# Top-2 experts: every expert on every token, or each token to its two experts only

## The chip, the cores and the metric

The kernel runs on one core of a Trainium2 chip. Times are device microseconds (us) of that core for one execution. The time before is the median of 3 runs, 867.42 us (864.79 to 869.43). The profile is of one further execution.

## The reference

The input is x, 8 sequences of 512 tokens with 128 features, all in float32. One causal attention layer with 16 heads of 8 features is followed by a layer normalization, then a mixture of 14 experts, then a second layer normalization:

```python
x = _layernorm(x + attention(x))          # 16 heads, head size 8, causal
t = x.reshape(4096, 128)
probs = softmax(t @ gate_w.T)             # (4096, 14)
top2_p, top2_i = top_k(probs, 2)
w = top2_p / top2_p.sum(-1)
hh = gelu(einsum('nd,edf->nef', t, w1) + b1)      # F = 256, exact gelu
all_out = einsum('nef,efd->ned', hh, w2) + b2     # all 14 experts
moe = w[:, 0] * all_out[n, top2_i[:, 0]] + w[:, 1] * all_out[n, top2_i[:, 1]]
x = _layernorm(x + clip(t + moe, -100, 100))
```

Only two of the 14 expert outputs of a token have a weight; the reference computes all and picks two.

## The kernel before

**Layout.** Tokens are tiles of 128 on the partitions: NQ = 4 tiles to a sequence, NT = 32 in all. The input x_sb, the attention result y_sb and all weights stay on chip. SP's queue carries the loads in the order of the code: x_sb (L71), the expert weights w1_sb and w2_sb (L101, L102), then everything that attention moves. The small weights and biases go on ScalarE's queue (L68 to L95). GpSimd (POOL) sets constants at the start.

**Attention** is written in an order of its own, by `tc.manual_schedule()`: instructions stay in program order on each engine. A unit u is four heads of one sequence, so there are NU = 32 units, 4 to a sequence, and a unit is UN = 5 steps. A loop over steps s calls `front(u, i)` for step s and `back(u, i)` for step s - 12 (LAG). Everything else is put on a step by `at(step, fn, ...)` into the table `jobs` and called after front and back of that step. `front` computes scores (L287) and a mask (L297) into PSUM and takes row maxima on VectorE. `shift_pieces` and `shift_rows` (L350 to L364) send the maxima as three bf16 rows into the operand qr, by a transfer on SP. `back` recomputes the transposed scores with the shift (L376), takes the exponential on ScalarE (L411), and POOL sets the masked part to zero (`select`, L387). `product` (L433) multiplies with the values, two or three steps after `back`. `evacuate`, `divide`, `project` and `residual` finish a unit or a sequence: the last adds the projection to x (L497) and takes the statistics of the layer normalization (L157, L158). `load_xT`, `split` (L248 to L260) and `load_rows` (L270, L277) prepare the next sequence: queries and keys are split into three bf16 pieces, stored to a scratch in DRAM and read back as rows.

**Experts.** After the last sequence, `layernorm_rstd` computes all scales at once, and a loop over the 8 sequences normalizes (L564), transposes (L572) and computes the router's logits (L575). The choice of the two experts is made for all 32 tiles in some 20 VectorE operations (L594 to L617) that end in w_all, a weight for every token and expert, zero for all but two. Then two nested loops, over 8 sequences c and 14 experts e, call `expert_in` (two matmuls L649 of 128 by 512 and two GELUs L653) one expert ahead of `expert_out` (eight matmuls L661 of 128 by 128, accumulated in PSUM in pairs, and four multiply-adds L669 on VectorE into acc). In the trace every float32 matmul is two entries (two passes), so L661 counts 1,792 and L649 448. `start` adds the biases b2 through a matmul (L633), `end` clips, adds, and takes statistics. After the last expert the second normalization runs over all tiles (L711), and SP stores each sequence (L719).

Of the kernel before, what the change touches and what calls it, by code (L numbers as in the profile page):

```python
# [12 lines left out]
BF = mybir.dt.bfloat16  # L13

# [14 lines left out]
LOWEST = -3.0e38  # L29


@with_exitstack
def kernel(
# [24 lines left out]
    SCALE = 1.0 / float(D) ** 0.5  # L58

# [37 lines left out]
    w1_sb = const.tile([P, E, F], FP, tag="w1_sb", name="w1_sb")  # L97
    w2_sb = const.tile([P, E, NFC, D], FP, tag="w2_sb", name="w2_sb")
    half = E // 2
    for lo, hi in ((0, half), (half, E)):  # L100
        nc.sync.dma_start(w1_sb[:, lo:hi, :], w1[lo:hi].rearrange("e d f -> d e f"))  # L101
        nc.sync.dma_start(  # L102
            w2_sb[:, lo:hi, :, :].rearrange("p e c d -> p (e c) d"),
            w2[lo:hi].rearrange("e (c p) d -> p (e c) d", p=P),
        )


    eps = const.tile([P, 1], FP, tag="eps", name="eps")
    nc.gpsimd.memset(eps, LN_EPS)
# [17 lines left out]
    for e in range(E):  # L127
        nc.gpsimd.memset(rank[:, e : e + 1], float(E - e))

# [20 lines left out]
    y_sb = const.tile([P, NT, D], FP, tag="y_sb", name="y_sb")  # L150
# [9 lines left out]
    def layernorm_rstd(pool, n):  # L160
        std = pool.tile([P, NT], FP, tag="std", name=f"std_{n}", bufs=1)
        rstd = pool.tile([P, NT], FP, tag="rstd", name=f"rstd_{n}", bufs=1)
        nc.scalar.activation(std, stats[:, :, 1], AF.Sqrt, bias=eps)
        nc.vector.reciprocal(rstd, std)
        return rstd
# [10 lines left out]
    with tc.tile_pool(name="work", bufs=2) as work, tc.tile_pool(  # L176
# [309 lines left out]
        def residual(b):  # L486
            aT, xb = outs.pop(("a", b))
            op = bank(f"op_{b}")
            for qb in range(NQ):
# [8 lines left out]
                y_sb[:, b * NQ : (b + 1) * NQ, :].rearrange("p t d -> p (t d)"),  # L498
                op,
                xb.rearrange("p t d -> p (t d)"),  # L500
                ALU.add,
            )
            for qb in range(NQ):
                layernorm_stats(work, y_sb[:, b * NQ + qb, :], b * NQ + qb)


        def step_of(u, i):
            return u * UN + i

# [11 lines left out]
        for u in range(NU):  # L521
# [10 lines left out]
            if g == NG - 1:  # L532
                at(k + 9, project, b)
                at(k + 11, residual, b)

        last = max(jobs)
        for s in range(-1, last + 1):
# [8 lines left out]
    with tc.tile_pool(name="big", bufs=1) as big, tc.tile_pool(  # L546
        name="ffn", bufs=2
    ) as ffn, tc.tile_pool(
        name="ps_t", bufs=2, space=bass.MemoryType.PSUM
    ) as ps_t, tc.tile_pool(  # L550
# [143 lines left out]
        for c in range(B):  # L694
            for e in range(E):
                hT = expert_in(c, e)
                if e == 0:
                    start(c)
# [66 lines left out]
```

## Time and profile before

| what | value |
|---|---|
| median of 3 runs | 867.42 us |
| the profiled execution | 868.49 us |
| its span, first to last instruction | 866.8 us |
| TensorE matmul busy | 775.2 us (89%) |
| TensorE weight load busy | 491.8 us (57%) |
| VectorE busy | 440.4 us (51%) |
| ScalarE busy | 372.0 us (43%) |
| POOL busy | 170.3 us (20%) |
| mean granted TensorE clock | 0.953 |
| DRAM read, written | 25.09 MB, 8.39 MB |

PE is TensorE's matmul, PEld its weight load, DVE VectorE, ACT ScalarE, POOL GpSimd, and SPq or ACTq the issue of a transfer on that queue. A group of instructions reads: line, engine, operation, output<-input, sizes, count | busy us, mean ns of one | idle us of the engine just before them, with what ended it. A matmul's own duration overlaps its neighbour's, so the beat of a repeated group in the chain says more than its mean. A stretch table gives the busy time of every engine between two times, and after it the granted clock (1.00 is full speed), the share of the DMA engines in use and GB/s.

### The profile page before, as it was taken

The numbers are of one execution on the slowest core, as the hardware profiler recorded it, in microseconds if no ns is written. First come the engines' busy times: TensorE is split into PE (matmuls) and PEld (weight loads), VectorE is DVE, ScalarE is ACT, GpSimd is POOL, SyncE is SP. The second block draws the span as 40 slices with busy tenths as digits, with TensorE's granted clock in tenths as the row PEclk, the third lists the DMA queues.
The fourth block names the chain that finished last, engine by engine and source line by source line (L and its number), as shares of the span: only waits on it lengthen the run. The fifth ranks groups of instructions, "written<-read, shape, count | busy, mean of one in ns | idle before, by whom it ended". The sixth has DMA issues, their size and how long they took to land.

```text
span 866.8 us, 13255 instructions
## 1 busy us (share of the span) xinstructions
PE 775.2 (89%) x5118; PEld 491.8 (57%) x5118; DVE 440.4 (51%) x996; ACT 372.0 (43%) x497; POOL 170.3 (20%) x455
## 2 busy tenths in 40 slices
PE   1489989989898999998698999999999999999992
PEld 0244444545454454554475777777777777777772
DVE  5275765666766674773446343434334343433436
ACT  0025544455565654567352443333333334344331
POOL 3133534354444443444100000000000000000000
PEclk9969997999999996999698999999999999999996
DMA  8531213122222221110000000000000000000003
GB/s 234 165 117 52 89 49 92 57 65 79 66 67 71 75 75 48 56 30 2 2 1 1 1 1 1 1 0 1 1 1 1 1 1 1 1 1 1 1 1 97
DMA packets 31060, 34.72 MB, mean 40 GB/s; under 512 B 5812, under 2 KB 26390, under 8 KB 30998
## 3 DMA queue, kind: packets, MB, share of 16 engines
q1 hardware_dynamic: 29632, 33.44, 12.8%
q8 instruction: 40, 0.66, 0.3%
q10 hardware_dynamic: 1366, 0.45, 0.2%
q14 instruction: 22, 0.18, 0.1%
HBM read 25.09 MB, written 8.39 MB: 39 GB/s over the span
## 4 chain that ended last, share of the span: by engine, by line
PE 84%; DVE 6%; ACT 4%; DMA 2%; issue 2%; POOL 1%; SPq 0%; ACTq 0%; POOLq 0%; DVEq 0%
PE op L661 23%; PE hp L649 21%; PE f L287 10%; PE av L433 9%; PE b L376 9%; PE f L297 3%; ACT pt L411 2%; PE tr L450 1%; PE op L490 1%; PE bp L633 1%; PE logits_ps L575 1%; DVE x_sb L711 1%; PE q L248 1%; DMA gate_nat<-in_L_ffn_gate_w_dram 1%; PE mt L360 1%
## 5 line engine op out<-in xcount | busy, mean ns | idle before, releaser
L653 ACT ACTIVATE hT<-hp,b1T 128x512 f32<-128x512 f32 x224 | 153.6, 687 | 247.9 <-PE hp L649 222.8
L661 PEld LDWEIGHTS op<-w_sb,hT 128*128 128x128 f32 x1792 | 218.1, 192 | 53.2 <-issue 30.1
L669 DVE SCALAR_TENSOR_TENSOR acc<-op,w_all,acc 128x128 f32<-128x128 f32 x448 | 126.0, 344 | 227.0 <-PE op L661 227.0
L661 PE MATMUL op<-w_sb,hT 128*128 128x128 f32 x1792 | 219.1, 275 | 0.0
L411 ACT ACTIVATE pt<-b 128x1024 f32<-128x1024 f32 x160 | 163.4, 1023 | 129.4 <-PE b L376 125.5
L649 PE MATMUL hp<-yT,w_sb 128*128 128x512 f32 x448 | 211.7, 595 | 0.4 <-ACT hT L653 0.4
L287 PE MATMUL f<-kr,qr 72*128 72x384 bf16 (+3 forms) x512 | 122.2, 323 | 8.4 <-DMA qr<-qsc 8.4
L387 POOL TENSOR_SCALAR_AFFINE_SELECT pt<-pt 128x256 f32<-128x256 f32 (+1 forms) x224 | 95.2, 439 | 157.5 <-ACT pt L411 144.6
L334 DVE TENSOR_REDUCE part<-f 128x8 f32<-128x1024 f32 x64 | 78.3, 1224 | 62.2 <-PE f L297 61.1
L649 PEld LDWEIGHTS hp<-yT,w_sb 128*128 128x128 f32 x448 | 76.9, 192 | 55.2 <-issue 53.2
L287 PEld LDWEIGHTS <-qr 72*128 72x128 bf16 x512 | 47.9, 103 | 103.8 <-issue 84.3
L376 PE MATMUL b<-qr,kr 75*128 75x384 bf16 (+3 forms) x512 | 100.8, 311 | 0.4
L433 PE MATMUL av<-pt,v_aug 128*32 128x512 f32 (+3 forms) x1024 | 94.2, 464 | 0.9 <-POOL pt L387 0.9
L341 DVE TENSOR_REDUCE mx<-f 128x2 f32<-128x1024 f32 x64 | 78.0, 1221 | 31.0 <-PE f L297 31.0
L297 PE MATMUL f<-causal_bf,ident_bf 128*128 128x256 bf16 (+1 forms) x320 | 85.8, 268 | 0.0
L376 PEld LDWEIGHTS <-kr 75*128 75x128 bf16 x512 | 46.2, 101 | 22.6 <-issue 8.3
L433 PEld LDWEIGHTS av<-pt,v_aug 128*32 128x32 f32 x1024 | 24.2, 111 | 42.0 <-issue 26.6
L329 DVE TENSOR_REDUCE mx<-f 128x4 f32<-128x1024 f32 x32 | 39.0, 1219 | 11.6 <-PE f L297 11.6
L297 PEld LDWEIGHTS <-ident_bf 128*128 128x128 bf16 x320 | 33.2, 104 | 12.3 <-issue 3.2
L360 PE MATMUL mt<-ident_bf,mp 128*48 128x128 bf16 x32 | 7.3, 227 | 28.4 <-DVE krest L252 12.6
L443 ACT COPY oT<-av 128x512 f32<-128x512 f32 x32 | 18.7, 584 | 19.2 <-PE av L433 19.1
L450 PE MATMUL tr<-ident,oT 128*128 128x128 f32 x128 | 20.6, 286 | 1.2 <-ACT oT L443 1.2
(109 smaller groups left out, 402.8 us busy)
## 6 DMA issues: line engine op xcount, KB each, us to landing
kr<-ksc SPq DMA_DIRECT2D x32, 288.0 KB
qr<-qsc SPq DMA_DIRECT2D x96, 96.0 KB
w_sb<-in_L_ffn_w_dram SPq DMA_DIRECT2D x4, 896.0 KB
qsc<-qpc SPq DMA_DIRECT2D x24, 128.0 KB
ksc<-kpc SPq DMA_DIRECT2D x24, 128.0 KB
x_sb<-in_L_attn_x_dram SPq DMA_DIRECT2D x8, 256.0 KB
out_dram<-x_sb SPq DMA_DIRECT2D x8, 256.0 KB
qr<-mt SPq DMA_DIRECT2D x96, 4.0 KB
```

What stands on the lines that cost most here:

```text
L287: nc.tensor.matmul(ps[:, col : col + W], qr[u % RING][0:KR, j, qb * P : (qb + 1) * P], kr[u % RING][0:KR, j, :W], start=first, stop=False, ...
L297: nc.tensor.matmul(out, ident_bf, causal_bf[:, 0:n, :], start=False, stop=True, skip_group_check=True,)
L334: nc.vector.reduce_max(part[:, j : j + 2, :], ps.rearrange("p b (s k) -> p b s k", k=P), axis=AX.X,)
L341: nc.vector.reduce_max(mx[:, j : j + 2, 3], ps, axis=AX.X)
L376: nc.tensor.matmul(ps[:, col : col + W], kr[u % RING][:, j, kb * P : (kb + 1) * P], qr[u % RING][:, j, kb * P :], start=first, stop=True, ...
L387: nc.gpsimd.affine_select(out=view, in_=view, pattern=[[0, k] for k in n] + [[1, P]], compare_op=ALU.is_ge, fill=0.0, base=0, channel_mult ...
L411: nc.scalar.activation(pt, ps, AF.Exp, scale=SCALE)
L433: nc.tensor.matmul(avs[u][HS * j : HS * (j + 1), kb * P :], v_aug[b % 2][:, kb, g * GH + j, :], p, start=(kb == 0), stop=(kb == NQ - 1),)
L649: nc.tensor.matmul(hp, w1_sb[:, e, f * P : (f + 1) * P], yT[:, c, :], start=True, stop=True)
L653: nc.scalar.activation(hT[:, f, :], hp, AF.Gelu, bias=b1T[:, k : k + 1])
L661: nc.tensor.matmul(op[:, i, :], hT[:, f, i * P : (i + 1) * P], w2_sb[:, e, f, :], start=(f == 0), stop=(f == NFC - 1),)
L669: nc.vector.scalar_tensor_tensor(acc[:, i, :], op[:, i, :], w_all[:, c * NQ + i, e : e + 1], acc[:, i, :], op0=ALU.mult, op1=ALU.add,)
```

## The change

Each token's row goes to its two experts only, through DRAM.

- **Routing per sequence.** `route(b)` is a generator; `proceed` runs one piece of it per step, from two steps after `residual` of that sequence. It normalizes on ScalarE (scale and shift from POOL), transposes, computes logits, takes the two best experts on VectorE, and counts with small matmuls (a strictly lower triangle and ones) at which row of its expert each token stands, with the running counts in `place`. The weights of the two experts come from one exponential and a power on POOL.
- **Scatter.** Each row is 130 numbers: 128 features, the weight, and where the result goes. Eight indirect transfers per sequence (4 tiles, 2 choices), each of 128 rows, go from POOL's queue into XS in DRAM, two per step.
- **Fill.** After the second to last sequence is counted, SP loads 14 places into registers and writes 768 rows behind each expert's rows, so that whole blocks can be read. The last sequence's first scatter waits for these.
- **Weights.** The expert weights aren't loaded on chip any more; at step 5 SP copies them within DRAM into WP, 514 numbers to a row, with the biases b1 at the end.
- **Blocks.** A plan on VectorE gives each of NBLK = 45 blocks of 256 tokens its first row in XS, its expert and how many of its rows count. SP loads row and expert of a block into registers and then its tokens and weights, four blocks ahead. A block is transposed, multiplied, passed through GELU, multiplied again, weighted on VectorE and scattered by two indirect transfers of 128 rows from POOL to OS; rows that don't count have a place outside and are left out.
- **End.** OS is read back in two halves per sequence, by SP and ScalarE. POOL adds the first, VectorE the second, and the rest is done for each sequence: clip, sum, statistics, scale on POOL, normalization on ScalarE, store.

The diff, cut to its core:

```diff
-    w1_sb = const.tile([P, E, F], FP, tag="w1_sb", name="w1_sb")
-    w2_sb = const.tile([P, E, NFC, D], FP, tag="w2_sb", name="w2_sb")
...
+    NBLK = (2 * N + E * (BT - 1)) // BT
...
+    def layernorm_scale(pool, c, n):
...
+        nc.gpsimd.tensor_scalar(rstd, stats[:, ts, 1], LN_EPS, 1.0, ALU.add, ALU.mult)
+        nc.gpsimd.tensor_tensor(rstd, rstd, powers[:, 0], ALU.pow)
+        nc.gpsimd.tensor_tensor(shift, stats[:, ts, 0], rstd, ALU.mult)
+        nc.gpsimd.tensor_scalar(shift, shift, -1.0, 0.0, ALU.mult, ALU.add)
...
+    def scatter(key, dst, idx, src, bound):
+        inst = nc.gpsimd.indirect_dma_start(
+            dst,
+            bass.IndirectOffsetOnAxis(ap=idx, axis=0),
+            src,
+            None,
+            bounds_check=bound,
+            oob_is_err=False,
+        )
...
+        def pack_weights():
+            wide = WP.rearrange("(e p) w -> e p w", p=P)
+            nc.sync.dma_start(WP[:, 0:F], w1.rearrange("e p f -> (e p) f"))
+            for c in range(NFC):
+                nc.sync.dma_start(
+                    wide[:, :, F + c * D : F + (c + 1) * D], w2[:, c * P : (c + 1) * P, :]
+                )
...
+                nc.sync.dma_start(
+                    wide[:, :, F + NFC * D :].rearrange("e p c -> p e c"),
+                    b1T.rearrange("p (e c) -> p e c", c=NFC),
+                )
...
+        def route(b):
...
+            rstd, shift = layernorm_scale(work, b, 0)
+            for i in range(NQ):
...
+                nc.scalar.activation(
+                    y_sb[:, t, 0:D],
+                    y_sb[:, t, 0:D],
+                    AF.Identity,
+                    bias=shift[:, i : i + 1],
+                    scale=rstd[:, i : i + 1],
+                )
+            yield
...
+            nc.vector.tensor_tensor(place, place, pp[:, NQ * E : (NQ + 1) * E], ALU.add)
+            if b == B - 2:
...
+                for e in range(E):
+                    to = nc.sync.value_load(
+                        place_i[0:1, e : e + 1], min_val=e * CAP, max_val=e * CAP + N
+                    )
+                    inst = nc.sync.dma_start(
+                        XS[bass.ds(to, PAD * P), :].rearrange("(p s) w -> p s w", s=PAD),
+                        y_sb[:, 0:PAD, :],
+                    )
...
+            for i in range(NQ):
+                for k, src in enumerate((y_sb[:, b * NQ + i, :], second[:, i, :])):
+                    inst = scatter("XS", XS[:, :], to_i[:, k, i : i + 1], src, E * CAP - 1)
+                    if b == B - 1 and i + k == 0:
+                        after_scatters(inst, "fill")
+                yield
...
+        at(5, pack_weights)
...
+                at(k + 13, proceed, k + 13, route(b))
...
+        def load(i):
+            at_row = nc.sync.value_load(
+                where[0:1, 0, i : i + 1], min_val=0, max_val=E * CAP - BT
+            )
+            at_w = nc.sync.value_load(where[0:1, 1, i : i + 1], min_val=0, max_val=(E - 1) * P)
+            xb = ffn.tile([P, SB, PW], FP, tag="xb", name=f"xb_{i}", bufs=6)
+            inst = nc.sync.dma_start(
+                xb, XS[bass.ds(at_row, BT), :].rearrange("(s p) w -> p s w", p=P)
+            )
+            if i == 0:
+                after_scatters(inst, "XS")
+            wt = ffn.tile([P, WW], FP, tag="wt", name=f"wt_{i}", bufs=6)
+            nc.sync.dma_start(wt, WP[bass.ds(at_w, P), :])
...
+        def expert_out(i):
...
+            for s in range(SB):
...
+                nc.vector.tensor_scalar(
+                    ob[:, s, :], op[:, s, :], xb[:, s, D : D + 1], 0.0, ALU.mult, ALU.add
+                )
+                scatter("OS", OS[:, :], to_i[:, s : s + 1], ob[:, s, :], 2 * N - 1)
...
+        AHEAD = 4
+        for i in range(-AHEAD, NBLK):
+            if i + AHEAD < NBLK:
+                load(i + AHEAD)
+            if 0 <= i + 2 < NBLK:
+                turn(i + 2)
+            if 0 <= i + 1 < NBLK:
+                expert_in(i + 1)
+            if i >= 0:
+                expert_out(i)
+                if i % 4 == 2 and i // 4 < B:
+                    biases(i // 4)
...
+        for c in range(B):
+            ts = slice(c * NQ, (c + 1) * NQ)
+            a = acc[:, ts, :]
+            nc.gpsimd.tensor_tensor(a, a, got[c][0], ALU.add)
+            nc.vector.tensor_tensor(a, a, got[c][1], ALU.add)
+            nc.vector.tensor_scalar(a, a, CLIP, -CLIP, ALU.min, ALU.max)
+            nc.vector.tensor_tensor(z_sb[:, ts, :], a, y_sb[:, ts, 0:D], ALU.add)
...
+            rstd, shift = layernorm_scale(ffn, c, 1)
```

## The prediction

> **What bounds the kernel now.** The page's chain of work that ended last comes first, by line:
>
> ```profile
> PE op L661 23%; PE hp L649 21%; PE f L287 10%; PE av L433 9%; PE b L376 9%; PE f L297 3%; ACT pt L411 2%; PE tr L450 1%; PE op L490 1%; PE bp L633 1%; PE logits_ps L575 1%; DVE x_sb L711 1%; PE q L248 1%; DMA gate_nat<-in_L_ffn_gate_w_dram 1%; PE mt L360 1%
> ```
>
> TensorE holds 84% of the chain, and its two largest items, L661 and L649, are the dense expert layers. The costliest groups say how much work that is (busy time, mean ns of one, then the idle time before and its releaser):
>
> ```profile
> L653 ACT ACTIVATE hT<-hp,b1T 128x512 f32<-128x512 f32 x224 | 153.6, 687 | 247.9 <-PE hp L649 222.8
> ...
> L669 DVE SCALAR_TENSOR_TENSOR acc<-op,w_all,acc 128x128 f32<-128x128 f32 x448 | 126.0, 344 | 227.0 <-PE op L661 227.0
> L661 PE MATMUL op<-w_sb,hT 128*128 128x128 f32 x1792 | 219.1, 275 | 0.0
> ...
> L649 PE MATMUL hp<-yT,w_sb 128*128 128x512 f32 x448 | 211.7, 595 | 0.4 <-ACT hT L653 0.4
> ...
> L387 POOL TENSOR_SCALAR_AFFINE_SELECT pt<-pt 128x256 f32<-128x256 f32 (+1 forms) x224 | 95.2, 439 | 157.5 <-ACT pt L411 144.6
> ```
>
> The reader is to see that ScalarE and VectorE wait for TensorE here (222.8 and 227.0 us), while TensorE waits for nothing. The chain in order of time gives the beat:
>
> ```profile
> 480.79 1.78 PE op L661 x16
> 484.29 1.78 PE op L661 x16
> ```
>
> One expert on one sequence takes 3.50 us, whatever the router said, and 8 x 14 = 112 of them take 392 us. The table of stretches (columns: length, then busy time and count of PE, PEld, DVE, ACT, POOL, then granted clock, DMA share, GB/s) shows the rest:
>
> ```profile
> 48.00:52.00 4.00, 1.13 (x5) 0.26 (x4) 3.43 (x4) 0.91 (x2) 2.48 (x7) 0.94 0.36 120
> 52.00:56.00 4.00, 4.00 (x19) 2.35 (x18) 2.79 (x4) 0.04 (x1) 1.44 (x3) 0.50 0.23 70
> 135.00:140.00 5.00, 3.39 (x25) 1.83 (x21) 2.17 (x4) 2.20 (x4) 3.11 (x9) 1.00 0.23 77
> 200.00:300.00 100.00, 90.11 (x768) 48.63 (x767) 68.65 (x97) 57.24 (x72) 44.59 (x118) 1.00 0.24 71
> 420.00:440.00 20.00, 14.31 (x59) 11.49 (x60) 10.88 (x42) 7.55 (x11) 0.00 (x0) 0.57 0.00 1
> 600.00:800.00 200.00, 200.00 (x1133) 144.42 (x1132) 76.01 (x273) 76.95 (x112) 0.00 (x0) 1.00 0.00 1
> 845.00:867.00 22.00, 5.91 (x42) 4.76 (x40) 14.36 (x55) 2.98 (x4) 0.00 (x0) 0.70 0.34 95
> ```
>
> Attention (200 to 300 us) is also TensorE's at 90%, with POOL at 45% and VectorE at 69%. From 420 to 440 the global normalization leaves TensorE at clock 0.57. In the experts POOL and DMA do nothing at all: that is where the change puts its work. The last 16 us are normalization and stores:
>
> ```profile
> 855.29 8.29 DVE L711 TENSOR_SCALAR x_sb<-x_sb,stats,rstd 128x128 f32<-128x128 f32 x32
> 856.44 7.54 SPq L719 DMA_DIRECT2D out_dram<-x_sb  x8
> ```
>
> **What is removed.** From 425 us (last attention statistics, line L158 in the timeline) to the end at 866.8 us everything is replaced: 442 us. The weights' 3.67 MB no longer go to SBUF ahead of attention.
>
> **Start.** In the timeline q (L248) begins at 21.46 us because the gate weights, issued at 11.26, land only at 18.4 among the weight transfers. Without these I put the landing at 13.5, so attention starts 5 us sooner. But the same 3.67 MB now go DRAM to DRAM from SP at step 5, with 1,792 eight-byte pairs of biases behind them. At 235 GB/s (first 22 us of the trace) that is 16 us plus a few, ahead of the first maximum rows that the second half of attention needs at step 12. I charge 5 us (0 to 15). The new small operations on POOL and VectorE before attention lie under the 18 us wait. Start: 0.
>
> **Attention.** A sequence takes 45.4 us there (the same product matmuls at 200.94 and 246.31), or 2.27 us for each of 20 steps. Into seven of the eight go:
> - TensorE: 4 transposes (0.53 us, by 1.07 for 8 at 442.41), 4 logit matmuls in 8 passes (0.96 us for 8 at 444.21), 5 small counting matmuls (about 0.1 each, by the 0.1 us weight load they need): 2.0 us each, 14 us, all on the path since TensorE is full.
> - VectorE: some 18 operations of 56 to 112 elements, at 0.19 each 3.4 us; ScalarE 4 normalizations at about 0.3, one 0.59 copy, one exponential: 2 us. Both engines have the room in sum (31 of 45 and 26 of 45 busy). Each queues ahead of a maximum or exponential that TensorE needs, so I charge 1 us a sequence: 7 us.
> - POOL: some 16 small operations at 0.2 and a 0.61 copy, 4 us, and 8 scatters in pairs over four steps. This is the unknown price, X.
>
> **The price X of a scatter.** The trace has no indirect transfer. The nearest rows are issues (start, time taken, queue):
>
> ```profile
> 0.80 0.43 ACTq L68 DMA_DIRECT2D wnat<-in_L_attn_Wq_dram  x1
> ...
> 0.81 7.83 SPq L71 DMA_DIRECT2D x_sb<-in_L_attn_x_dram  x8
> ```
>
> One of 128 rows takes 0.43 us, one of 512 rows 7.83/8 = 0.98, both with the address in the instruction; a list read by POOL costs more, so 0.45 is the lower end. The Trainium skill ("DMA: Bandwidth & Descriptors", Anatomy of one DMA — SWDGE (gpsimd) path) fits 2.0 us + bytes/436e3 to a DMA issued by POOL, 2.15 for 64 KB, which speaks against the change if POOL were held for all of it. It also says that most of the 2 us is the write receipt, during which the queue goes on. So 2.15 is my upper end, and I take 1.4, an estimate near the middle. With X = 1.4 a scatter step costs POOL 0.7 (selects) + 2.8 against 2.27: after four steps it is 4.9 us late. The masked probabilities of L387 are then late for the product, queued behind the scatters. The last of them has about 1.5 steps, 3.3 us, of slack; 1.6 us come through per sequence, 11 us in all. By 2.15 it would be 53, by 1.0 nothing.
>
> Attention thus ends at 425 + 0 + 14 + 7 + 11 = 457.
>
> **Last sequence.** Nothing covers its routing. POOL scale 1.1, ScalarE 1.3, transposes 0.7, copy 0.6, logits 1.2, twelve VectorE operations 2.6, count 0.75, places 0.9, POOL's weight operations 2.3 (these stand ahead of the scatters), twelve hand-overs at 0.15: 13.3 us. Then 8 X = 11.2, landing 2.5 (nearest: 2.0 for ksc in the chain): block loads start at 484. The planning (some 30 small VectorE operations, 6 us) runs beside the scatters. The 14 fills of 400 KB (5.6 MB, 24 us at 235 GB/s; SP issues them in about 20) start some ten steps earlier and should be just done; no charge, up to 5 us if they are not. First block to its output: 2.7 load + 5 through the engines, 492.
>
> **Forty-five blocks.** Per block:
> - TensorE: 8 output passes of 128 columns at 1.78/16 = 0.111, 4 passes of 256 at half of 1.72/4 (1.72 is what L649's four passes of 512 leave of the 3.50), two transposes at 0.15: 0.89 + 0.86 + 0.30 = 2.05 us.
> - ScalarE 2 x 0.45 and VectorE 1.4: hidden.
> - DMA: 133 KB rows + 263 KB weights + 131 KB scattered, 527 KB at 235 GB/s: 2.24 us.
> - SP: two loads of a register and two transfers. The transfers by the issue rows (256 and 128 rows) 0.62 + 0.45. For a register load there is no row near: its lower end is 0.2 (the shortest VectorE operations), and the skill's same page (Latency and other measured facts) gives it a floor of about 0.6; the upper end I put at twice that. I take 0.7, and 0.4 for the six small checks around them: 2.9.
> - POOL: 2 X = 2.8.
>
> I take the largest and a little, 3.0 us, or 135 us, to 627. The biases (8 times 1.3 us of TensorE) fit into its free 0.95.
>
> **The end.** Last scatter and first load back: 5.5 us. Then POOL's queue decides. It holds, per sequence, the first addition (1.27, L478) and four small operations that need VectorE's statistics, and the next addition stands behind them. VectorE (0.69 + 0.43 + 0.69 + 4 x 0.445 = 3.6) needs that addition. So the engines take turns: 1.27 + 3.6 + 1.1 + hops = 6.1 us, eight times 49. Then ScalarE and the store, 5: 686. This end is 60 us where the old one was 16.
>
> Span 686, time of the profiled execution 688 (868.49 stood 1.7 over its span); the median of the runs shown is 1 us below that execution, so **687**.
>
> **The clock.** TensorE will be 70% busy in the blocks. The skill ("TensorE: Matmul & The Clock Gate", HAM oscillation — how this bites in real kernels) warns that idle gaps over some 3.4 us bring the half clock. The stretches agree on both sides: 28% busy at 48 to 52 is followed by 0.50, 68% at 135 to 140 keeps 1.00. Gaps of 1 us should keep it. By the rule with longer gaps, TensorE would need 4.1 us a block, 736 in all[...].
>
> **Rivals.**
> - Leaner: X = 1.0 and register loads of 0.2. The blocks fall to 2.25 (34 us less), the stall goes (11), the scatters give 3: 639. For it: DMA share is 0.24 in attention and 0 after it. Against: register use is never that free of checks.
> - POOL is the bound: X = 2.15. Blocks 4.3 (+58), attention +42, last scatters +6: 793.
> - Half clock or late buffers in the blocks: 736.
> - Slower than before: the same scatter, from X = 2.65 on. At 2.7: blocks 5.4 (+108), attention +73, scatters +10: 878. For it: 154 scatters on one queue, and nothing in the trace prices them. Against: six times the 128-row issue row.
> - No gain since the dense work stays: excluded, as the output matmuls fall from 896 to 180 in number.
>
> **How the numbers follow.** Likeliest case (650 to 730) 0.55; POOL bound 0.15; leaner 0.12; half clock 0.07; slower 0.10; chance meeting 0.01. Only the two cases under 640 and over 800 are cut: the range is 630 to 800. Faster by over 0.5%, about what a measurement of this kernel can tell from no change: 0.89; within 0.01; slower 0.10.
>
> **What would show it.** Scatter rows on POOL with mean near 1.4 us; blocks every 3.0 us with SP or POOL as releaser; TensorE's clock near 1 in the blocks; attention ending near 457; some 27 us between that and the first block load; a tail of 60 us in which POOL and VectorE alternate. Wrong if a scatter holds POOL over 2 us, if a register load takes over 1.2 us, or if the pack at step 5 stalls attention by more than 15.

## The result

The changed kernel takes 938.97 us (median of 4 runs, 931.75 to 944.15) where the kernel before takes 867.36 beside it: a ratio of 1.082, with an interval of 1.074 to 1.090. The forecast was 687. It was wrong in sign, and by 252 us. The profiled execution took 931.75 us; its span is 930.0 us against a predicted span of 686, so 244 us have to be found.

The chain of work that ended last, by engine and by line, of the changed kernel:

```profile
PE 39%; issue 15%; POOL 13%; DVE 11%; DMA 9%; ACT 7%; SPq 5%; POOLq 0%; ACTq 0%; DVEq 0%
PE av L506 8%; PE f L360 8%; PE b L449 8%; DMA OS<-ob,bto_i 5%; POOL OS L218 5%; ACT pt L484 3%; PE f L370 3%; PE o L902 3%; POOL rstd L205 2%; PE h L887 2%; DVE ob L909 2%; DMA wt<-WP 1%; POOL pt L460 1%; POOL XS L218 1%; SPq L584 1%
```

The dense layers are gone from it, as they should be: the two items that held 44% of the old chain have become 5%. But TensorE's share has fallen from 84% to 39%, and no other engine took its place. The rest is spread over issue, DMA, POOL and VectorE, and that is how a chain looks that runs from engine to engine through waits. The costliest groups say the same (busy time, mean ns, then the idle time before and its releaser):

```profile
L218 POOL DMA_INDIRECT OS<-ob,bto_i x90 | 87.3, 970 | 195.9 <-DVE ob L909 183.6
...
L902 PE MATMUL o<-wt,hT 128*128 128x128 f32 x360 | 86.2, 383 | 44.0 <-DVE ob L909 44.0
...
L891 ACT ACTIVATE hT<-h,wt 128x256 f32<-128x256 f32 x90 | 42.7, 474 | 215.6 <-PE h L887 179.5
...
L879 DVE CAST bto_i<-bto 128x2 int32<-128x2 f32 x45 | 7.6, 170 | 112.2 <-DMA OS<-ob,bto_i 112.1
```

Read them as a ring. POOL waits for VectorE (`ob`), TensorE waits for VectorE, ScalarE waits for TensorE, and VectorE, in a cast of 0.17 us, waits 112 us for a DMA. The table below has VectorE, ScalarE and POOL idle for two thirds of the blocks and more; TensorE is busy for 71% of them, but at a clock of 0.66 and with waits for VectorE. So none of them is the bound there. Note also the mean of the first row: a scatter holds POOL for 0.97 us, less than the 1.4 that the forecast took.

The table of stretches (length, busy time and count of PE, PEld, DVE, ACT, POOL, granted clock, DMA share, GB/s) for attention, the blocks and the end:

```profile
76.00:540.00 464.00, 374.50 (x2775) 193.56 (x2773) 252.64 (x442) 217.36 (x290) 235.96 (x557) 0.87 0.20 65
...
608.00:864.00 256.00, 180.52 (x634) 127.15 (x632) 61.38 (x231) 40.78 (x86) 86.45 (x90) 0.66 0.30 77
864.00:930.00 66.00, 0.00 (x0) 0.00 (x0) 26.94 (x88) 12.85 (x32) 23.25 (x41) 0.50 0.35 96
```

With the times of the same events in both kernels the 244 us can be placed. Predicted times follow from the steps of the forecast; the value product is L433 before and L506 after.

| event | before | predicted | measured | this stage adds |
|---|---|---|---|---|
| first value product | 66.6 | 66.6 | 82.6 | +16 |
| last value product | 416.8 | 448.8 | 527.0 | +62 |
| statistics of the last sequence done | 425 | 457 | 557.4 | +22 |
| first load of a block | - | 484 | 593.3 | +9 |
| first scatter of a block | - | 492 | 607.8 | +7 |
| last scatter of a block | - | 627 | 863.7 | +121 |
| end of the span | 866.8 | 686 | 930.0 | +7 |

Half of the error is the blocks, a quarter the beat of attention; the rest is in five smaller places. Each but one got an experiment. The 7 us too many between the first load and the first scatter of a block were not tried. The trace shows the order of the code there: three blocks are transposed and two are multiplied by their first weights before the output matmuls of the first block start, at 605.57.

### The profile page after: what moved, and what is told of

Read it like the earlier page. It is cut to its first block, busy times and chain, and to the rows that moved or that the text cites. A ratio compares the mean times of both kernels' runs of the same rounds, so it can differ in the third digit from the quotient of the medians.

```text
span 930.0 us, 11215 instructions
## 1 busy us (share of the span) xinstructions
PE 595.8 (64%) x3550; PEld 343.9 (37%) x3550; DVE 386.4 (42%) x866; ACT 282.3 (30%) x428; POOL 386.2 (42%) x779
## 4 chain that ended last, share of the span: by engine, by line
PE 39%; issue 15%; POOL 13%; DVE 11%; DMA 9%; ACT 7%; SPq 5%; POOLq 0%; ACTq 0%; DVEq 0%
PE av L506 8%; PE f L360 8%; PE b L449 8%; DMA OS<-ob,bto_i 5%; POOL OS L218 5%; ACT pt L484 3%; PE f L370 3%; PE o L902 3%; POOL rstd L205 2%; PE h L887 2%; DVE ob L909 2%; DMA wt<-WP 1%; POOL pt L460 1%; POOL XS L218 1%; SPq L584 1%
## 5 line engine op out<-in xcount | busy, mean ns | idle before, releaser
L218 POOL DMA_INDIRECT OS<-ob,bto_i x90 | 87.3, 970 | 195.9 <-DVE ob L909 183.6
L460 POOL TENSOR_SCALAR_AFFINE_SELECT pt<-pt 128x256 f32<-128x256 f32 (+1 forms) x224 | 95.4, 442 | 165.7 <-ACT pt L484 158.6
L449 PE MATMUL b<-qr,kr 75*128 75x384 bf16 (+3 forms) x512 | 107.6, 326 | 20.8 <-DMA qr<-mt 19.2
L902 PE MATMUL o<-wt,hT 128*128 128x128 f32 x360 | 86.2, 383 | 44.0 <-DVE ob L909 44.0
L891 ACT ACTIVATE hT<-h,wt 128x256 f32<-128x256 f32 x90 | 42.7, 474 | 215.6 <-PE h L887 179.5
L506 PE MATMUL av<-pt,v_aug 128*32 128x512 f32 (+3 forms) x1024 | 105.5, 500 | 1.5 <-POOL pt L460 0.9
L887 PE MATMUL h<-bxT,wt 128*128 128x256 f32 x180 | 84.8, 566 | 28.9 <-ACT hT L891 28.3
L902 PEld LDWEIGHTS o<-wt,hT 128*128 128x128 f32 x360 | 75.3, 276 | 60.6 <-DVE ob L909 55.2
L887 PEld LDWEIGHTS h<-bxT,wt 128*128 128x128 f32 x180 | 39.7, 273 | 55.7 <-ACT hT L891 54.4
L909 DVE TENSOR_SCALAR ob<-o,xb 128x128 f32<-128x128 f32 x90 | 31.4, 349 | 66.6 <-PE o L902 65.5
L879 DVE CAST bto_i<-bto 128x2 int32<-128x2 f32 x45 | 7.6, 170 | 112.2 <-DMA OS<-ob,bto_i 112.1
L506 PEld LDWEIGHTS av<-pt,v_aug 128*32 128x32 f32 x1024 | 25.5, 115 | 50.8 <-issue 36.7
L218 POOL DMA_INDIRECT XS<-y_sb,to_i x32 | 32.9, 1029 | 26.0 <-DMA XS<-y_sb 17.4
```

The costliest lines, as they stand in the source:

```text
L218: inst = nc.gpsimd.indirect_dma_start(dst, bass.IndirectOffsetOnAxis(ap=idx, axis=0), src, None, bounds_check=bound, oob_is_err=False,)
L449: nc.tensor.matmul(ps[:, col : col + W], kr[u % RING][:, j, kb * P : (kb + 1) * P], qr[u % RING][:, j, kb * P :], start=first, stop=True, ...
L460: nc.gpsimd.affine_select(out=view, in_=view, pattern=[[0, k] for k in n] + [[1, P]], compare_op=ALU.is_ge, fill=0.0, base=0, channel_mult ...
L506: nc.tensor.matmul(avs[u][HS * j : HS * (j + 1), kb * P :], v_aug[b % 2][:, kb, g * GH + j, :], p, start=(kb == 0), stop=(kb == NQ - 1),)
L887: nc.tensor.matmul(hp[:, f, :], wt[:, f * P : (f + 1) * P], xT, start=True, stop=True)
L902: nc.tensor.matmul(op[:, s, :], hT[:, f, s * P : (s + 1) * P], wt[:, F + f * D : F + (f + 1) * D], start=(f == 0), stop=(f == NFC - 1),)
```

## Where the time went, in the trace

**Blocks.** The timeline of one beat (start, length, instruction, in brackets the idle time before it and its releaser):

```profile
703.74 0.17 DVE L879 CAST bto_i<-bto 128x2 int32<-128x2 f32 x1 [3.15 <-DMA OS<-ob,bto_i]
703.82 0.35 DVE L909 TENSOR_SCALAR ob<-o,xb 128x128 f32<-128x128 f32 x1
...
704.44 0.97 POOL L218 DMA_INDIRECT OS<-ob,bto_i  x1 [2.88 <-DVE ob L909]
...
706.10 0.97 POOL L218 DMA_INDIRECT OS<-ob,bto_i  x1 [0.70 <-DVE ob L909]
...
709.72 0.17 DVE L879 CAST bto_i<-bto 128x2 int32<-128x2 f32 x1 [3.33 <-DMA OS<-ob,bto_i]
```

From cast to cast is 5.98 us. The second scatter of the block starts 2.36 us after the cast, and the next cast comes 3.62 us after that, when the scatter has landed. `to_i`, the list of row numbers that a scatter reads, has the three buffers that its pool gives by default. The cast in `turn(i + 2)` needs the buffer of block i - 1, so it waits for that block's scatters. In VectorE's program the scaling `ob` of block i stands behind that cast, and in the trace it starts right after it (703.82 after 703.74). So the scatter of block i can't start before the scatter of block i - 1 has landed.

**Attention.** The output projection (L563) starts at 256.33 and at 317.85: 61.5 us for a sequence, where it was 45.4. TensorE's waits between 76 and 540 us (total, times, longest):

```profile
PE mt L433 <- ACT xT L297: 23.1, 6, 4.4
...
PE b L449 <- DMA qr<-mt: 19.2, 1, 19.2
```

The second is the start, of which more below. The first, in the timeline:

```profile
324.97 1.05 POOL L205 TENSOR_TENSOR rstd<-rstd,powers 128x4 f32<-128x4 f32 x1
...
326.61 1.65 ACT L606 ACTIVATE y_sb<-y_sb,shift,rstd 128x128 f32<-128x128 f32 x4 [2.83 <-POOL shift L207]
...
328.16 1.00 ACT L484 ACTIVATE pt<-b 128x1024 f32<-128x1024 f32 x1
329.07 0.57 ACT L297 COPY xT<-xt 128x512 f32<-128x512 f32 x1
...
329.69 0.26 PE L433 MATMUL mt<-ident_bf,mp 128*48 128x128 bf16 x1 [4.38 <-ACT xT L297]
```

The statistics are done at 321.5, but POOL reaches the scale only behind its masks, and the power of four columns takes 1.05 us. ScalarE, which came to the normalization at 323.8, waits for it with an exponential and a copy behind it that TensorE needs. TensorE stands still for 4.4 us, and its clock over attention is 0.87, where the kernel before has 0.95:

```profile
60.00:422.00 362.00, 328.08 (x2655) 172.57 (x2654) 227.05 (x324) 200.54 (x248) 153.96 (x406) 0.95 0.20 60
```

**Last sequence.** The timeline once more, some lines of it:

```profile
543.77 1.14 POOL L218 DMA_INDIRECT XS<-y_sb,to_i  x1 [17.41 <-DMA XS<-y_sb]
...
555.15 0.69 DVE L570 TENSOR_TENSOR y_sb<-op,xb 128x512 f32<-128x512 f32 x1 [25.89 <-POOL xb L551]
...
583.98 0.17 DVE L794 TENSOR_TENSOR count<-place,base_e 128x14 f32<-128x14 f32 x1 [14.65 <-issue]
...
593.34 0.43 SPq L860 DMA_DIRECT2D xb<-XS  x1
```

The scatters of the second to last sequence write to the same tensor as the fills, which SP issues from 524.4 to 540.4, and so they wait for them, 17.4 us. POOL's addition `xb` for the last sequence (L551, 1.3 us) is queued behind these eight scatters, and VectorE waits 25.9 us for it. Later the plan (from L794) starts only at 584, when the last scatters have gone, and the loads come 9 us after it starts.

## The experiments

Each of the first six undoes one suspected wait in the changed kernel and leaves everything else; none leaves out a part of the output. The runs of the changed kernel lie 12 us apart (931.75 to 944.15), so a gain below that is read from the waits in the trace and not from the total.

**Eight buffers for the row numbers.**

```diff
-            to_i = ffn.tile([P, SB], I32, tag="to_i", name=f"bto_i_{i}")
+            to_i = ffn.tile([P, SB], I32, tag="to_i", name=f"bto_i_{i}", bufs=8)
```

> Theory A, the blocks' beat is set by the reuse of the index tile: it has 3 buffers, so the index of block i+2 (VectorE) waits until both scatters of block i-1 have landed and read theirs, and the weighting of block i stands behind that wait in VectorE's queue. With 8 buffers that wait goes: the beat falls from 5.8 to 2.3 to 3.2 us (2.05 us of TensorE at full clock, 2.4 of SP, 2.5 of POOL), the clock in the blocks rises from 0.67 to over 0.9, and the time from 939 to 800 to 825. Theory B, the beat is set by the weights' transfers and the half clock (TensorE 4.1 us at half clock, transfers at a third of the DMA engines' time): the beat stays over 4.5 and the time over 880.

Measured: 855.54 us (854.84 to 855.84), ratio to the kernel before 0.985 (0.983 to 0.988). One number takes off 83 us and brings the kernel 1.5% under the one before. The cast no longer waits for a landing, the blocks run from 613.8 to 787.4, and TensorE's clock there is 0.98:

```profile
614.00:787.00 173.00, 121.49 (x634) 86.64 (x633) 62.33 (x231) 40.72 (x86) 86.15 (x89) 0.98 0.44 115
```

The steady beat is 3.57 us, the mean 3.95. Theory A is right on the wait and the clock, but the beat is longer and the total 30 us higher than it said. The timeline shows what is left of it:

```profile
692.68 0.71 PE L902 MATMUL o<-wt,hT 128*128 128x128 f32 x4 [0.45 <-DVE ob L909]
692.91 0.97 POOL L218 DMA_INDIRECT OS<-ob,bto_i  x1 [3.09 <-DVE ob L909]
...
694.66 0.70 PE L887 MATMUL h<-bxT,wt 128*128 128x256 f32 x2 [0.61 <-ACT hT L891]
...
696.25 0.71 PE L902 MATMUL o<-wt,hT 128*128 128x128 f32 x4 [0.45 <-DVE ob L909]
```

TensorE stops twice in each beat: the second half of h waits for the GELU of the first half, and the second half of o for the scaling of the first. Both halves share a tile in PSUM, and the code has the reader of the first half ahead of the writer of the second.

**The weight copies ahead of attention.** The three large copies of L582 and L584 move from step 5 to a place right behind the loads of x; the bias pairs stay.

```diff
+    wide = WP.rearrange("(e p) w -> e p w", p=P)
+    nc.sync.dma_start(WP[:, 0:F], w1.rearrange("e p f -> (e p) f"))
+    for c in range(NFC):
+        nc.sync.dma_start(
+            wide[:, :, F + c * D : F + (c + 1) * D], w2[:, c * P : (c + 1) * P, :]
+        )
...
     def scatter(key, dst, idx, src, bound):
...
         def pack_weights():
...
-            nc.sync.dma_start(WP[:, 0:F], w1.rearrange("e p f -> (e p) f"))
-            for c in range(NFC):
```

> Only the bulk copies of the weights within DRAM move, from step 5 of attention to right behind the input's loads on SP's queue, where the kernel before loads its weights; the 14 KB of biases stay. Theory A, SP's queue was held 12 us by these issues and the first maximum rows came 19 us late: the first value product starts at 66 to 74 instead of 82.6, and the time falls by 9 to 17 to 922 to 930. Theory B, the bias pairs (5.9 us of issue) or the engines' transfer rate held it: the start stays over 78 and the time at 939.

Measured: 937.02 us (932.5 to 941.55). The total is as theory B has it, the start as theory A: the first value product comes at 73.9 instead of 82.6. The copies now delay the gate weights: TensorE waits 15.9 us for them, where in the changed kernel it had not waited for them at all. What became of the 9 us isn't shown. From the first to the last value product it is 449.6 us here and 444.4 in the changed kernel, but 448 to 452 in the seven other experiments that leave attention's order as it is, so this difference may be the spread of the runs.

**The scale one step before the normalization.**

```diff
             rstd, shift = layernorm_scale(work, b, 0)
+            yield
             for i in range(NQ):
```

> One more step lies between POOL's scale of a sequence and ScalarE's use of it; the arithmetic is the same. Theory A, ScalarE stands 2.8 us for POOL's power, TensorE waits 4.4 and 5.2 us for ScalarE's copies behind it and then runs at half clock: a sequence falls from 61.5 to 50 to 55 us, the clock in attention rises from 0.87 to over 0.92, and the time falls by 40 to 75 to 864 to 899. Theory B, the added work itself (POOL's scatters, VectorE's small operations) costs the 16 us: a sequence stays at 58 or more, the time over 915.

Measured: 883.55 us (882.79 to 884.32), ratio 1.018 (1.014 to 1.021). One word takes off 55 us: the scale is issued on POOL one step before ScalarE asks for it. The addition ahead of the statistics (L570) comes every 52.4 us instead of 61.5, the clock over attention is 0.95 again, and TensorE's wait for that copy is 6.9 us in all, the longest 1.1:

```profile
76.00:480.00 404.00, 349.23 (x2767) 182.74 (x2766) 249.56 (x442) 214.86 (x290) 235.55 (x557) 0.95 0.22 67
```

```profile
PE mt L433 <- ACT xT L297: 6.9, 6, 1.1
```

Theory A. The first and the last value product are now 394 us apart, which is 44 more than before the change; the forecast had 32.

**Scatters of the second to last sequence without the fills.** The fills write rows that no scatter of that sequence touches, so its scatters are declared not to depend on them.

```diff
                     inst = scatter("XS", XS[:, :], to_i[:, k, i : i + 1], src, E * CAP - 1)
+                    if b == B - 2:
+                        tc.declare_no_dep(inst.ins, group="fill", reason="rows below those")
```

> The scatters of the second to last sequence no longer wait for the fills, whose rows lie behind theirs. Theory A, that wait held POOL 17 us and with it the last sequence's first operation on POOL: the last sequence's statistics end near 535 instead of 557, and the time falls by 15 to 22 to 917 to 924. Theory B, the last sequence's own scatters have to wait for the fills anyway: the gain is under 8.

Measured: 918.64 us (916.23 to 921.06), 20 us less: theory A. The wait of 17.4 us is gone. The scatters start at 532.49, and `xb` still comes behind all eight of them:

```profile
542.57 1.28 POOL L551 TENSOR_TENSOR xb<-x_sb,bo_bc 128x512 f32<-128x512 f32 x1
543.89 0.69 DVE L570 TENSOR_TENSOR y_sb<-op,xb 128x512 f32<-128x512 f32 x1 [8.69 <-POOL xb L551]
```

**POOL's additions at the end in one go.** The tiles that OS is read back into get eight buffers instead of four with it, so that all can be there.

```diff
-                o = ffn.tile([P, NQ, D], FP, tag=f"o{k}", name=f"o{k}_{c}", bufs=4)
+                o = ffn.tile([P, NQ, D], FP, tag=f"o{k}", name=f"o{k}_{c}", bufs=8)
...
+        for c in range(B):
+            a = acc[:, c * NQ : (c + 1) * NQ, :]
+            nc.gpsimd.tensor_tensor(a, a, got[c][0], ALU.add)
         for c in range(B):
...
-            nc.gpsimd.tensor_tensor(a, a, got[c][0], ALU.add)
```

> The eight additions of GpSimd at the end (L966) are issued together before the loop of the last normalization, so that none stands behind the scale chain of the sequence before it (o tiles get eight buffers). Theory A (the alternation of GpSimd between its addition and its scale chain sets the period of 6.9 us of the end): from the last scatter to the end 66 us become 40 to 50, the total falls by 16 to 26 us to 912 to 923. Theory B (VectorE's own work of a sequence, or the loads of OS, set it): the end stays at 60 to 66 us and the total within 4 us of 938.

Measured: 922.03 us (921.23 to 922.83). From the last scatter (871.87) to the end of the span (919.5) it is 47.6 us instead of 66.3, 19 less; the total falls by 17. Theory A. VectorE's wait for the additions, in the changed kernel first and then in this one (total, times, longest):

```profile
DVE acc L967 <- POOL acc L966: 31.5, 8, 8.8
```

```profile
DVE acc L969 <- POOL acc L965: 8.8, 1, 8.8
```

POOL and VectorE took turns, as the forecast had it, and they needn't have: only the first addition is still waited for.

**Memory of its own for the plan.** The plan's tiles come from the pool of the constants and not from one that takes over attention's memory.

```diff
-            return plan.tile([P, n], dt, tag=name, name=name)
+            return const.tile([P, n], dt, tag=f"p_{name}", name=f"p_{name}")
...
```

> The plan's tiles get memory of their own, so that they do not wait for memory that the last scatters of attention still read. Theory A (the plan of 9 us stands behind the landing of the scatters only through that memory): the plan runs beside the last scatters, the loads of the blocks start 7 to 11 us earlier, the total falls to 926 to 933. Theory B (the fill of counts in the last sequence itself ends late, or the loads wait for the scatters in any case as long): the total stays within 4 us of 938.

Measured: 932.64 us (930.67 to 934.6), 6 us less, within theory A's range, but the runs of the two kernels overlap. The trace is clearer. The plan's first operation now starts at 573.61 and its last at 582.07, beside the scatters. Here are the last scatter into XS and the first load of a block, in the changed kernel (the load is shown above) and in this one:

```profile
580.44 0.97 POOL L218 DMA_INDIRECT XS<-second,to_i  x1 [0.30 <-DMA XS<-second,to_i]
```

```profile
585.41 0.97 POOL L218 DMA_INDIRECT XS<-second,to_i  x1 [0.30 <-DMA XS<-second,to_i]
...
588.34 0.43 SPq L860 DMA_DIRECT2D xb<-XS  x1
```

From the one to the other it was 12.9 us and is 2.9. So all of the plan's 9 us came back in this stage, and what is left is the landing of the scatters, for which SP waits 5 us. The load comes only 5 us earlier by the clock of the profile because this execution was 5 us later before the last scatters.

**The matmuls of a block ahead of their readers**, with the eight buffers:

```diff
                 nc.tensor.matmul(
                     hp[:, f, :], wt[:, f * P : (f + 1) * P], xT, start=True, stop=True
                 )
+            for f in range(NFC):
                 c = F + NFC * D + f
...
+            for s in range(SB):
                 nc.vector.tensor_scalar(
                     ob[:, s, :], op[:, s, :], xb[:, s, D : D + 1], 0.0, ALU.mult, ALU.add
                 )
```

> Eight buffers for the row numbers of the scatter back, as in e1_toi8, and in addition both matmuls of h ahead of both GELUs, and all four matmuls of o ahead of both scalings. Theory A (in e1_toi8 the second matmul of h waits for the GELU of the first half and the second half of o for the scaling of the first, 1.06 us of TensorE's time per block): the beat falls from 3.57 us to TensorE's busy time of 2.3 to 2.8, the total from 855.5 to 806 to 828. Theory B (SP's issues with their register loads, or the landing of the transfers, set 3.57): the beat stays at 3.3 to 3.6 and the total at 843 to 857.

Measured: 795.33 us (790.44 to 797.36), ratio 0.915 (0.910 to 0.920). It is 60 us less than with the buffers alone, and the total lies below the range of theory A, which counted from the steady 3.57 where the mean was 3.95. The blocks take 114.4 us, 2.55 each. And it isn't TensorE that sets this beat, as the expectation had it:

```profile
691.53 0.97 POOL L218 DMA_INDIRECT OS<-ob,bto_i  x1 [0.30 <-DVE bto_i L879]
692.81 0.97 POOL L218 DMA_INDIRECT OS<-ob,bto_i  x1 [0.30 <-DVE ob L911]
694.08 0.97 POOL L218 DMA_INDIRECT OS<-ob,bto_i  x1 [0.30 <-DVE bto_i L879]
```

Scatter follows scatter every 1.28 us, 0.97 busy and 0.30 between, whichever releaser is named. For 38 of these gaps the profile shows nothing that POOL waited for, and the same 0.30 us stand between its scatters into XS. POOL is the bound, 2 x 1.28 = 2.55 a block. TensorE is busy 95.4 of 115 us, 2.1 a block, which is the 2.05 of the forecast.

**Four buffers, and the new order alone.** Two kernels for how the two edits depend on each other: `bufs=4` and nothing else; and the diff just shown with the three buffers as they were.

> Four buffers for the row numbers of the scatter back instead of three, nothing else. Theory A (with three, the cast for block i+2 waits for the landing of block i-1's scatter and holds up the scaling of block i, so one landing stands in every beat of 5.98 us; a fourth puts two beats between): the beat falls to about 3.6 us and the total to 851 to 862, as with eight buffers. Theory B (the landings pile up over many blocks, and only many buffers help): the beat stays above 4.5 us and the total above 885.

> The order of e8_split (both matmuls of h ahead of both GELUs, all four of o ahead of both scalings), but three buffers for the row numbers as in the changed kernel. Theory A (the loop through the landing rules: landing 3.6 us from the second scatter's start, cast, scalings 0.6, 1.3 to the second scatter): the beat goes from 5.98 to about 5.5 us, the total from 938 to 912 to 924, much less than the 60 us the same edit gave on top of eight buffers. Theory B (the hand-overs count in full in either kernel): the total falls by 45 to 65 us to 873 to 893.

Measured: four buffers 848.23 us (847.18 to 849.29), so one more buffer does all that eight do (theory A; the total is 3 us below its range). The new order alone 900.21 us (897.39 to 903.04): 39 us, which lies between the two theories. The timeline has the loop through the landing as theory A says, VectorE's cast idle for it in each beat:

```profile
692.49 0.17 DVE L879 CAST bto_i<-bto 128x2 int32<-128x2 f32 x1 [3.65 <-DMA OS<-ob,bto_i]
...
697.23 0.17 DVE L879 CAST bto_i<-bto 128x2 int32<-128x2 f32 x1 [3.66 <-DMA OS<-ob,bto_i]
```

but a beat of 4.74 and not 5.5 us, because the landing was shorter: 2.74 us from the second scatter's start (689.75) to the cast, where it was 3.62 in the changed kernel (medians over the blocks 2.7 and 3.5). Why it was shorter isn't settled.

**All together.** The eight buffers, the new order, the early scale, the scatters free of the fills, the additions in one go and the plan's own memory:

> e3_scale_early, e4_nofill, e5_adds_first, e6_plan_const and e8_split in one kernel. If the causes add up (each counted with its own run or expectation: 939 - 55 - 20 - 20 - 9 - 131): about 704, with 695 to 730 as the range. If one hides another (the plan beside the scatters, the fills beside the last sequence): 730 to 760.

Measured: 700.68 us (695.72 to 702.8), ratio 0.806 (0.801 to 0.810). From 938.97 the single gains 143.6 (buffers and order), 55.4, 20.3, 16.9 and 6.3 add to 242.5, or 696.5; measured is 238.3. The gains add up to within 4 us, less than the spread of the runs, so the waits were separate.

**Early copies on top of that.** The edit of the second experiment in this kernel:

> e9_best with the bulk of the weight copies moved to the front as in e2_pack_early. Theory A (the early copies did shorten the start by 9 us in e2_pack_early, and the gain was lost later to the waits that e9_best has removed): 688 to 696. Theory B (the copies cost the same wherever they stand, since something else is late in their place): 697 to 705.

Measured: 711.58 and 732.47, both above the 700.68 without the edit and outside both theories' ranges, and too far apart for a size. Only the run of 732.47 has a profile, so nothing is explained from it. That the early copies gain nothing here either is all that these runs show.

**The last wait for `xb`.** On top of the kernel with all six, the addition `xb` is issued eleven steps earlier, ahead of the scatters of the sequence before:

```diff
+                at(k - 2, add_bias, b)
                 at(k + 9, project, b)
```

> e9_best with GpSimd's addition of the output bias to x (xb, L551 of the changed kernel) issued eleven steps earlier, ahead of the scatters of the sequence before. Theory A (in the last sequence the 9.7 us that VectorE waits for xb lie on the path that sets the end): the blocks start 7 to 10 us earlier and the total is 689 to 696. Theory B (the landing of the last fills or scatters is what the first block waits for, whatever the last sequence does): 698 to 703.

Measured: 689.66 us (687.18 to 696.86), ratio 0.795 (0.789 to 0.801), 11 us less by the medians: theory A. The runs of the two kernels meet (695.72 is the lowest without this edit), and the profiled executions, 696.86 and 700.62, show less. VectorE's wait before that addition (L570, here L574) goes from 9.73 to 3.63, and it is then TensorE that it waits for; before and after:

```profile
497.23 0.69 DVE L570 TENSOR_TENSOR y_sb<-op,xb 128x512 f32<-128x512 f32 x1 [9.73 <-POOL xb L551]
```

```profile
490.73 0.69 DVE L574 TENSOR_TENSOR y_sb<-op,xb 128x512 f32<-128x512 f32 x1 [3.63 <-PE op L567]
```

The first scatter of a block comes at 533.8 instead of 537.9. So the trace shows 4 to 6 of the 11 us. This is the fastest version: it beats the kernel before by 20%.

## Why the prediction was wrong

**Forty-five blocks: "I take the largest and a little, 3.0 us".** This step failed, and it costs 121 us. It took the largest of five busy times as the beat, which holds if nothing ties one block to the next. Something did: the buffer of the row numbers, held until a scatter has landed. The times themselves were good or high: TensorE 2.05 (measured 2.1 where it runs at full clock), POOL 2.8 (2.55), SP 2.9 (2.27 from the issue of one block's rows at 595.69 to that of the next at 597.96, while nothing held it; a register load is 0.27 us and 0.15 for its arithmetic, not 0.7, and less than half of the floor of 0.6 that the forecast cites). The beat was 5.8 to 6.0 because landing, cast, scaling and issue stood in a row. The page of the Trainium skill that the price of a scatter came from ("DMA: Bandwidth & Descriptors", Anatomy of one DMA — SWDGE (gpsimd) path) fits some 2.0 us and the bytes to one such DMA, setup and completion together, most of it the write receipt; for 64 KB that is an estimate of 2.15. The trace has 0.97 us on POOL, and a median of 3.3 us from issue to landing in this kernel. So X, read from that page, was two quantities. The forecast asked how long POOL is held; who is held until the landing was the question that decided.

**Attention: "so I charge 1 us a sequence: 7 us".** Failed: the beat is 61.5 us, not 45.4 + 4.6. Both engines had the room in sum, as the step says, but ScalarE comes to the normalization before POOL has the scale, and what it has queued behind is needed by TensorE. The early scale shows it: with it, the stretch between the first and the last value product is 50 us shorter, of the 62. That POOL would be late through the scatters (11 us) had the price wrong: by 0.97, or 1.27 with the gap behind each, the forecast's own working gives 0 to 4 us. With the early scale attention is still 12 us over the forecast's 32; what these 12, and those not spent on scatters, went to was not tried.

**Start: "Start: 0".** Failed by 16 us. Attention did start sooner, q at 18.25 instead of 21.46, 3 of the 5 us; but TensorE then waited 19.2 us for the maximum rows. SP's queue holds the copies in order, before the first maximum rows (`mt`, needed at step 12):

```profile
48.35 10.15 SPq L584 DMA_DIRECT2D WP<-in_L_ffn_w_dram  x1
58.61 5.94 SPq L588 DMA_DIRECT2D WP<-b1T  x1
64.65 7.79 SPq L333 DMA_DIRECT2D ksc<-kpc  x3
72.52 1.87 SPq L437 DMA_DIRECT2D qr<-mt  x3
```

The copies take their time in the issue itself: of the three the first two are issued in 0.65 and 1.07 us, the third holds the queue for 10.15, the pairs for 5.94, and the three stores behind them take 7.79 us. With the early copies, where nothing large stands right before them, the pairs and the stores take much less, so they too were held by the copies:

```profile
57.28 0.54 SPq L590 DMA_DIRECT2D WP<-b1T  x1
57.92 3.32 SPq L340 DMA_DIRECT2D ksc<-kpc  x3
```

The forecast counted when the bytes would be through, and charged 5. Its text names 15 as the point from which it would be wrong. Moving the copies to the front took 9 us off the start in the trace, and nothing that the total shows.

**Last sequence: "no charge, up to 5 us if they are not".** The fills were late by 17.4 us. They start when the second to last sequence is counted, at 524, not ten steps before their use; and those that wait are the scatters of that same sequence, with `xb` of the last one in the queue behind them. 20 us came back by the declaration, and moving `xb` took off 11 by the medians, 4 to 6 in the trace. That the planning "runs beside the scatters" failed as well: 9 us, held up by memory and not by data, and all of them came back with memory of its own.

**The end** was right in its mechanism and 7 us too short: 59 us from 627 to 686, 66 measured, in turns of 6.9 us as against 6.1. The power took 1.04 us where other small operations on POOL take 0.2.

**The clock: "Gaps of 1 us should keep it".** In the changed kernel they did not. The granted clock over the blocks was 0.66, with TensorE busy 180.5 of 256 us (71%), and its waits for `ob` between 620 and 860 us were 1.0 us in the mean and 2.5 at most:

```profile
PE o L902 <- DVE ob L909: 41.3, 41, 2.5
```

With the eight buffers the clock was 0.98, with TensorE busy 121.5 of 173 us, 70%, and no wait over 0.61. The same share has both clocks, so the share doesn't decide. (Each share is counted at its own clock: at the full one the work of the blocks would fill some 47% of the 256 us, an estimate from the 121.5.) In the kernel before, too, TensorE is busy for 15.7 of the 16 us from 52 to 68 us, at 0.50. The rule weighed in the forecast ("TensorE: Matmul & The Clock Gate", HAM oscillation — how this bites in real kernels) puts the return to half clock at gaps over some 3.4 us; here shorter ones went with it. Yet the half clock is more a companion than the cause: the edit that took the wait away brought the clock back with it, and the landing alone is 3.6 of the 5.98 us. What the clock adds to the other 2.4 was not taken apart. That is also where the rival "half clock or late buffers" went wrong. It named late buffers and priced the half clock, 4.1 a block.

**Slower than before: "the same scatter, from X = 2.65 on".** Slower had its 0.10 through POOL's price alone; it came at a price of 0.97, so not by that rival's mechanism. The measured prices are near those of the "leaner" rival (X = 1.0, register loads of 0.2), which gave 639, but for the 0.30 us between two scatters, which neither had. The version with the waits gone has a span of 695.1, near the forecast's 686, but partly because errors cancel: up to the statistics of the last sequence (493 for 457) it is 36 us longer, from there to the first scatter (533.8) 6 longer, the blocks are 21 shorter (114 for 135) and the end 12 (47 for 59). The count of the work was fair; what it left out were the waits between its parts.

## What to carry to other kernels

Before taking the largest busy time as the beat of a loop, follow each buffer to the instruction that frees it: here the list of addresses given to an indirect transfer was held until that transfer had landed, and whatever stood behind the wait for it in the same engine's program went at the pace of that landing. When the chain shows every engine with a small share and a tiny instruction with a large idle time before it, look there first; one more buffer, one step between producer and consumer, or a writer moved ahead of a reader may be the whole difference (here all of them together led from 8% slower to 20% faster). And a small operation put on another engine's queue costs what that queue holds before it, and not only its own time: `xb` takes 1.3 us, and VectorE stood 25.9 us for it.

## What the hardware showed that was not expected

- An indirect scatter of 128 rows holds POOL for 0.97 us, and the next starts 0.30 us later; it lands 2.1 to 3.7 us after its issue in the changed kernel, 3.3 in the median (2.3 with eight buffers, and also in some of the experiments that keep three).
- A power of 128x4 takes POOL 1.04 us (median of 16), five times what its other operations of that size take (0.20).
- Copies within DRAM can hold SP's queue: of three issued in a row (1,792, 896 and 896 KB) the third took 10.15 us to issue, the first 0.65; small transfers behind them were held too (1,792 pairs of 8 bytes 5.94 us, and 0.54 where the copies came much earlier).
- Loading a number into a register of SP took 0.27 us (median of 45).
- TensorE ran at clock 0.66 and at 0.98 with the same busy share of 70%, with waits of up to 2.5 us in the one and up to 0.61 us in the other.
